# Last section of a one-core transformer kernel in a new order: TensorE transposes for the last tile, results of the last but one pair on ScalarE and GpSimd

## The chip, the cores and the metric

The kernel runs on one core of one Trainium2 chip. A core has five engines that run their own instruction streams side by side: TensorE (PE in the profile, with its weight loads as PEld), VectorE (DVE), ScalarE (ACT), GpSimd (POOL) and SyncE (SP), which here only issues DMAs. They meet through semaphores. PSUM is TensorE's accumulator memory; SBUF is the working memory. The metric is the device time of one execution in microseconds (us), as the median of several runs; lower is better.

## What is computed

The reference takes 64 sequences of 64 tokens of width 1024, adds an attention block to them, and then adds a quantized feed-forward block. Only the second part matters here:

```python
z   = x @ W.T + SCALING * lora(x)                # "cond2", 4096 tokens x 1024
def dynamic_quant(v, inv_smooth):                # one scale for each token
    s = v * inv_smooth
    scale = maximum(max(abs(s), axis=-1) / 127, 1e-8)
    return clip(round(s / scale), -127, 127), scale
qg, sg = dynamic_quant(bf16(z), inv_gate)        # over 1024 columns
qu, su = dynamic_quant(bf16(z), inv_up)
g = (qg @ w_gate.T) * sg * s_wgate               # 512 columns
u = (qu @ w_up.T)   * su * s_wup
inter = bf16(clip(silu(g) * u, -10, 10))
qi, si = dynamic_quant(inter, inv_inter)         # over 512 columns
out = x + (qi @ w_down.T) * si * s_wdown         # 1024 columns
```

## The kernel before

The 4096 tokens are 32 tiles of 128 tokens, and two tiles make a pair; there are 16 pairs. The second stage (`second_stage`) handles one pair after another, and the steps of neighbouring pairs are interleaved by hand. The order of the Python calls is the order of the instructions on each engine: the block runs under a manual schedule, so an instruction that waits holds up everything behind it on its engine. Semaphores follow from which tile each instruction reads and writes. A tile comes from a pool with a number of buffers for each tag, taken in turn; the first write into a buffer that is used again waits until every reader of the tile that had it before is done, and a DMA counts as done when it has landed.

The steps of one tile, with the lines that the profile gives them:

- `undivided` / `completed` (L1487, L1463): TensorE makes z in PSUM. `rounded` (L1497): ScalarE writes it to SBUF as bf16.
- `quant_a`: VectorE multiplies by the smoothing row (L1531), takes the largest absolute value (L1535), and `scaled_down` makes the scale and its reciprocal (L1559, L1561); ScalarE then rounds in two passes (L1562, L1564). `quant_half` / `quant_whole` (L1546, L1547, L1553) do the same for a tile whose two halves of 512 columns come at different times.
- `quant_b`: VectorE clips (L1572). The operand is then turned, either by a transposing DMA that SyncE issues (L1575) or, with `by_pe`, by TensorE into PSUM (L1579), from where ScalarE copies it (L1580).
- `gate_or_up` (L1589): eight matmuls. `scaled` (L1594): VectorE applies the scales, and for the gate ScalarE takes the sigmoid (L1600). `glu` (L1606, L1607, L1609): three VectorE instructions. Then `quant_a` and `quant_b` once more for "i", with 512 columns.
- `down` (L1619): two times four matmuls. `result` (L1628): VectorE multiplies a half tile from PSUM by the token's scale and the column scale in one instruction. Without an adder, GpSimd then issues an accumulating DMA of the whole tile into the output (L1636), where x already stands. With an adder, x is added from SBUF (L1632, on GpSimd or VectorE), and SyncE stores each half (L1633).

The change lies in the straight-line section at the end of the stage, from L1699. There p is the last pair, q the last but one, r the one before that. Names in the text such as "q0" or "p1" are a pair and its tile (0 or 1); "the last tile" is p1. When the stretch in question begins, at 2370.5 us of the span, TensorE has just finished the last base product (the second half of p1). What is left then: both operands of p1, their gate and up matmuls, the glu of p0 and p1, and the down matmuls and results of q0, q1, p0 and p1.

Buffers that the steps speak of: pool `q3` has two buffers for each tag. In the kernel before, the results of q0 and q1 use tag "y"; the results of p0 and p1 use tag "q", in which q_g and q_u of the last tile stood before them. In the new function `result_by_act` the results of q0 and q1 have tag "q" too. The PSUM pools `ps_g` and `ps_h` have four banks each.

Of the kernel before, what the change touches and what calls it, by code (L numbers as in the profile page):

```python
# [11 lines left out]
F32 = mybir.dt.float32  # L12
# [3 lines left out]
AF = mybir.ActivationFunctionType  # L16
ALU = mybir.AluOpType
AX = mybir.AxisListType
PSUM = bass.MemoryType.PSUM

P = 128
# [1264 lines left out]
def second_stage(tc, a, out_t, xT_d, ident, ps_g, KC, NT, H, C, half, comb, op):  # L1286


    nc = tc.nc
# [7 lines left out]
    hs = [slice(0, HH), slice(HH, H)]  # L1297

    with ExitStack() as ctx:
# [7 lines left out]
        def load_row(name, src, n, pool=None):  # L1307
            t = (pool or w).tile([P, n], F32, tag=name, name=name)
            nc.sync.dma_start(t, bcast_rows(src))
            return t  # L1310
# [35 lines left out]
        p2 = ctx.enter_context(tc.tile_pool(name="q3", bufs=2, reuse_waits="tile"))  # L1346
# [3 lines left out]
        st = st1  # L1350
# [12 lines left out]
        sd_w = load_row("sd_w", a["s_wdown"], H)  # L1363
# [131 lines left out]
        def rounded(p, t, n):  # L1495
            s = st[p]
            nc.scalar.copy(s["z"][:, t, hs[n]], s.pop(("ps", t, n)))  # L1497
# [22 lines left out]
            elif i == 3:  # L1520
                nc.vector.tensor_tensor(z[:, 1, hs[0]], ps, s.pop("u2"), ALU.add)

        def quant_a(p, t, nm, between=None):

            s = st[p]
            src, inv, n = {
                "g": (lambda: s["z"][:, t, :], ig, H), "u": (lambda: s["z"][:, t, :], iu, H),
                "i": (lambda: s.pop(("inter", t)), ii, I),
            }[nm]
            q = p2.tile([P, n], F32, tag="q" + ("i" if nm == "i" else ""), name=f"q_{nm}_{p}_{t}")  # L1530
            nc.vector.tensor_tensor(q, src(), inv, ALU.mult)  # L1531
            if between:
                quant_b(*between)
            am = sm.tile([P, 1], F32, tag="am" + nm, name=f"am_{nm}_{p}_{t}")
            nc.vector.tensor_reduce(am, q, AX.X, ALU.max, apply_absolute_value=True)  # L1535
            scaled_down(p, t, nm, q, am, n)

        def quant_half(p, t, nm, n):

            s = st[p]  # L1540
            inv = ig if nm == "g" else iu
            if n == 0:
                s["q", nm] = p2.tile([P, H], F32, tag="q", name=f"q_{nm}_{p}_{t}")
                s["am", nm] = sm.tile([P, 2], F32, tag="amh" + nm, name=f"amh_{nm}_{p}_{t}")
            q = s["q", nm][:, hs[n]]
            nc.vector.tensor_tensor(q, s["z"][:, t, hs[n]], inv[:, hs[n]], ALU.mult)  # L1546
            nc.vector.tensor_reduce(s["am", nm][:, n:n + 1], q, AX.X, ALU.max, apply_absolute_value=True)  # L1547

        def quant_whole(p, t, nm):
            s = st[p]  # L1550
            q, am2 = s.pop(("q", nm)), s.pop(("am", nm))
            am = sm.tile([P, 1], F32, tag="am" + nm, name=f"am_{nm}_{p}_{t}")
            nc.vector.tensor_tensor(am, am2[:, 0:1], am2[:, 1:2], ALU.max)  # L1553
            scaled_down(p, t, nm, q, am, H)

        def scaled_down(p, t, nm, q, am, n):
            s = st[p]
            sc = s["sc", nm, t] = sm.tile([P, 1], F32, tag="sc" + nm, name=f"sc_{nm}_{p}_{t}", bufs=4)
            nc.vector.tensor_scalar(sc, am, 1.0 / QMAX, 1e-8, ALU.mult, ALU.max)  # L1559
            rs = sm.tile([P, 1], F32, tag="rs" + nm, name=f"rs_{nm}_{p}_{t}")  # L1560
            nc.vector.reciprocal(rs, sc)  # L1561
            nc.scalar.activation(q, q, AF.Copy, bias=MAGIC, scale=rs)  # L1562
            qb = s["qb", nm, t] = p2.tile([P, n], BF16, tag="qb" + nm, name=f"qb_{nm}_{p}_{t}")
            nc.scalar.activation(qb, q, AF.Copy, bias=-MAGIC)  # L1564

        def quant_b(p, t, nm, by_pe=False):


            s = st[p]
            n = I if nm == "i" else H  # L1570
            qb = s.pop(("qb", nm, t))
            nc.vector.tensor_scalar(qb, qb, QMAX, -QMAX, ALU.min, ALU.max)  # L1572
            s["qT", nm, t] = qT = p2.tile([P, n // P, P], BF16, tag="qT" + nm, name=f"qT_{nm}_{p}_{t}")
            if not by_pe:
                nc.sync.dma_start(qT, qb, transpose=True)  # L1575
                return
            ps = ps_g.tile([P, n // P, P], BF16, tag="g", name=f"qTp_{nm}_{p}_{t}")
            for c in range(n // P):
                nc.tensor.transpose(ps[:, c, :], qb[:, c * P:(c + 1) * P], ident_b)  # L1579
            nc.scalar.copy(qT, ps)  # L1580

        def gate_or_up(p, t, nm):
            s = st[p]
            qT = s.pop(("qT", nm, t))

            pool, tag = (ps_g, "g") if (p, t) == (NPAIR - 1, 1) else (ps_h, "h")
            ps = s["pgu", nm, t] = pool.tile([P, I], F32, tag=tag, name=f"p{nm}_{p}_{t}")
            for k in range(KC):
                nc.tensor.matmul(ps, qT[:, k, :], wt_b["w" + nm][:, k, :], start=(k == 0), stop=(k == KC - 1))  # L1589

        def scaled(p, t, nm):
            s = st[p]
            o = p1p.tile([P, I], F32, tag="o" + nm, name=f"o{nm}_{p}_{t}")
            nc.vector.scalar_tensor_tensor(  # L1594
                o, s.pop(("pgu", nm, t)), s.pop(("sc", nm, t)), sg_w if nm == "g" else su_w, ALU.mult, ALU.mult
            )
            s["o", nm, t] = o
            if nm == "g":
                e = p1p.tile([P, I], F32, tag="e", name=f"e_{p}_{t}")
                nc.scalar.activation(e, o, AF.Sigmoid)  # L1600
                s["e", t] = e

        def glu(p, t):
            s = st[p]
            e, g, u = s.pop(("e", t)), s.pop(("o", "g", t)), s.pop(("o", "u", t))
            nc.vector.tensor_mul(e, g, e)  # L1606
            nc.vector.tensor_mul(e, e, u)  # L1607
            inter = p1p.tile([P, I], BF16, tag="inter", name=f"inter_{p}_{t}")
            nc.vector.tensor_scalar(inter, e, LIMIT, -LIMIT, ALU.min, ALU.max)  # L1609
            s["inter", t] = inter  # L1610

        def down(p, t):
            s = st[p]
            qT = s.pop(("qT", "i", t))
            for n in range(2):
                pool, tag = (ps_g, "g") if p == NPAIR - 1 else (ps_h, "h")
                ps = s["pd", t, n] = pool.tile([P, HH], F32, tag=tag, name=f"pd_{p}_{t}_{n}")
                for k in range(IC):
                    nc.tensor.matmul(  # L1619
                        ps, qT[:, k, :], wt_b["wd"][:, k, hs[n]], start=(k == 0), stop=(k == IC - 1)  # L1620
                    )

        def result(p, t, *adds):
            s = st[p]
            y = p2.tile([P, H], F32, tag="q" if p == NPAIR - 1 else "y", name=f"y_{p}_{t}")
            si = s.pop(("sc", "i", t))
            for n in range(2):
                nc.vector.scalar_tensor_tensor(  # L1628
                    y[:, hs[n]], s.pop(("pd", t, n)), si, sd_w[:, hs[n]], ALU.mult, ALU.mult
                )  # L1630
                if adds:
                    adds[n % len(adds)].tensor_add(y[:, hs[n]], y[:, hs[n]], s["x", t][:, hs[n]])  # L1632
                    nc.sync.dma_start(out_t[2 * p + t, :, hs[n]], y[:, hs[n]])  # L1633
            if not adds:

                nc.gpsimd.dma_start(out_t[2 * p + t], y, accum_op=ALU.add)  # L1636

        def do(when, f, *args):
# [5 lines left out]
        for p in range(NPAIR - 1):  # L1644
            q, r = p - 1, p - 2
# [6 lines left out]
            do(last, down, r, 0)  # L1652
            token_sums(p)
            do(last, quant_a, r, 1, "i")
            base(p, 1)
            after(p, 1)
# [42 lines left out]
        p, q, r = NPAIR - 1, NPAIR - 2, NPAIR - 3  # L1699
# [44 lines left out]
        glu(q, 1)  # L1744
        gate_or_up(p, 0, "g")
        rounded(p, 1, 1)
        quant_half(p, 1, "g", 0)
        quant_half(p, 1, "u", 0)
        gate_or_up(p, 0, "u")
        quant_half(p, 1, "g", 1)  # L1750
        quant_whole(p, 1, "g")
        quant_b(q, 0, "i")
        quant_half(p, 1, "u", 1)
        quant_whole(p, 1, "u")
        down(q, 0)
        quant_b(p, 1, "g")
        quant_a(q, 1, "i")
        scaled(p, 0, "g")
        scaled(p, 0, "u")
        quant_b(p, 1, "u")  # L1760
        gate_or_up(p, 1, "g")
        glu(p, 0)
        quant_b(q, 1, "i")
        gate_or_up(p, 1, "u")
        quant_a(p, 0, "i")
        scaled(p, 1, "g")
        scaled(p, 1, "u")
        down(q, 1)
        quant_b(p, 0, "i", True)
        glu(p, 1)  # L1770
        quant_a(p, 1, "i")
        result(q, 0)
        down(p, 0)
        quant_b(p, 1, "i", True)
        result(q, 1, nc.gpsimd)
        result(p, 0, nc.gpsimd, nc.vector)
        down(p, 1)
        result(p, 1, nc.vector)
# [54 lines left out]
```

## Time and profile before

| | us |
|---|---|
| median of 3 runs | 2402.47 (2402.36 to 2408.15) |
| the execution that was profiled, its own time | 2406.19 |
| its span, first to last instruction | 2404.4 |
| TensorE busy | 2367.6 (98% of the span) |
| VectorE busy | 1334.5 (56%) |
| ScalarE busy | 936.2 (39%) |
| GpSimd busy | 418.7 (17%) |
| end of the last base product | about 2370.5 |
| end of the last VectorE instruction | 2397.71 |

Start times below are counted from the start of the span. A timeline row gives the start, the duration, the engine, the line of the kernel, the operation, and output and inputs by the program's names, with shapes; in brackets stands how long the engine had been idle before it and what ended that.

### The profile page before, as it was taken

Reading aid. Unit: us, or ns where it says so; the run is one execution under the profiler, and the core shown is the slowest. Engines: PE = TensorE matmul, PEld = TensorE weight load, DVE = VectorE, ACT = ScalarE, POOL = GpSimd, SP = SyncE. Lnnn points to the kernel's source line nnn. Section 1 sums busy time; section 2 is a strip of 40 time slices with the busy share of each in tenths; the row PEclk is TensorE's granted clock in tenths of the full one; section 3 lists DMA queues with packets and bytes.
Section 4 is the critical chain, followed back from the end, with each engine's and each line's share of the span. In section 5 each row is a group of like instructions: output and inputs, shape, how many; then the busy total and the mean of one; then the engine's idle time right before and its main releaser. Section 6 shows DMA issues by size and latency. Waiting matters only on the chain.

```text
span 2404.4 us, 41907 instructions
## 1 busy us (share of the span) xinstructions
PE 2367.6 (98%) x17066; PEld 1628.5 (68%) x17104; DVE 1334.5 (56%) x2584; ACT 936.2 (39%) x1220; POOL 418.7 (17%) x470
## 2 busy tenths in 40 slices
PE   8999999999999999999999999999999999999997
PEld 7888888888888888888888444444454545454452
DVE  3573474464543644633535533324377878777787
ACT  1344344343344443443434544343333333333333
POOL 4121112111122223220000333334100000000000
PEclk9999999999999999999999999999999999999999
DMA  7899799899899998997967788877733443444353
GB/s 229 217 240 248 190 228 241 221 232 220 208 232 274 212 255 230 242 237 179 207 188 196 213 257 258 275 218 248 239 77 75 90 79 83 84 86 82 70 119 76
DMA packets 612395, 453.84 MB, mean 189 GB/s; under 512 B 362465, under 2 KB 524258, under 8 KB 606690
## 3 DMA queue, kind: packets, MB, share of 16 engines
q1 hardware_dynamic: 581522, 393.91, 63.2%
q0 software_dynamic: 12240, 40.38, 7.9%
q10 hardware_dynamic: 18432, 16.79, 3.1%
q8 instruction: 137, 2.24, 0.4%
q14 instruction: 64, 0.52, 0.1%
HBM read 274.02 MB, written 91.23 MB: 152 GB/s over the span
## 4 chain that ended last, share of the span: by engine, by line
PE 92%; DMA 2%; DVE 1%; SPq 1%; issue 1%; ACT 0%; ACTq 0%; DVEq 0%
PE poa L1129 5%; PE poc L1129 5%; PE pod L1129 5%; PE psvc L530 4%; PE psva L530 4%; PE psvd L530 4%; PE pbc L1129 4%; PE pbd L1129 4%; PE pba L1129 4%; PE pskc L509 4%; PE pskd L509 4%; PE pska L509 4%; PE psqa L509 4%; PE psqd L509 4%; PE psqc L509 4%; PE pr L1398 2%
## 5 line engine op out<-in xcount | busy, mean ns | idle before, releaser
L582 ACT ACTIVATE prob<-prob 128x512 f32<-128x512 f32 x128 | 80.6, 629 | 346.7 <-DVE prob L578 338.6
L608 ACT COPY pT<-phT 128x1024 int16<-128x1024 int16 x128 | 165.4, 1339 | 25.4 <-DMA phT<-ph 21.4
L596 ACT COPY ph<-prob 128x1024 int16<-128x1024 int16 x128 | 133.5, 1043 | 63.1 <-DVE prob L590 38.4
L442 POOL COPY yB<-yhT 128x512 int16<-128x512 int16 (+1 forms) x84 | 75.8, 955 | 426.4 <-DMA yhT<-yh 426.4
L1636 POOL DMA_DIRECT2D out_dram<-y x29 | 25.2, 869 | 656.2 <-DVE y L1628 644.4
L577 DVE TENSOR_REDUCE mx<-s 128x8 f32<-128x512 f32 x128 | 87.4, 682 | 71.6 <-PE s L568 71.6
L1250 POOL TENSOR_TENSOR xo<-xo,ob 128x1024 f32<-128x1024 f32 x32 | 83.5, 2629 | 228.2 <-DVE prob L578 189.5
L509 PE MATMUL psqa<-yB,wq 128*128 128x256 f32 x512 | 121.1, 379 | 0.5 <-ACT psqp L479 0.5
L509 PE MATMUL pska<-yB,wk 128*128 128x256 f32 x512 | 120.9, 379 | 0.0
L1224 ACT COPY xh<-xo 128x1024 int16<-128x1024 int16 x64 | 64.4, 1041 | 142.8 <-DVE xo L1269 142.8
L530 PE MATMUL psva<-wv,yB 128*128 128x256 f32 x512 | 115.8, 379 | 0.0
L1129 PE MATMUL poa<-woA,cx 128*128 128x512 f32 x256 | 115.3, 593 | 0.0
L1129 PE MATMUL pba<-wtA,x1T 128*128 128x512 f32 x240 | 107.9, 592 | 0.0
L1235 ACT COPY xTo<-xhT 128x1024 int16<-128x1024 int16 x64 | 84.7, 1337 | 58.4 <-DMA xhT<-xh 53.3
L530 PEld LDWEIGHTS psva<-wv,yB 128*128 128x128 f32 x512 | 97.2, 190 | 14.0 <-issue 0.8
L509 PEld LDWEIGHTS psqa<-yB,wq 128*128 128x128 f32 x512 | 97.1, 190 | 14.0 <-ACT psqp L479 0.9
L509 PEld LDWEIGHTS pska<-yB,wk 128*128 128x128 f32 x512 | 97.3, 190 | 13.2
L633 ACT ACTIVATE co<-banks,bqkv 128x256 f32<-128x256 f32 x128 | 60.7, 474 | 109.3 <-PE banks L411 79.8
L1266 POOL TENSOR_TENSOR xo<-xo,ou 128x512 f32<-128x512 f32 x48 | 59.9, 1275 | 191.8 <-DVE ou L1263 191.8
L590 DVE TENSOR_TENSOR prob<-prob,den 128x512 f32<-128x512 f32 x128 | 89.4, 699 | 4.4
L578 DVE TENSOR_TENSOR prob<-s,mx 128x512 f32<-128x512 f32 x128 | 88.5, 691 | 4.5
L1129 PEld LDWEIGHTS poa<-woA,cx 128*128 128x128 f32 x256 | 48.5, 190 | 60.0 <-issue 59.5
(255 smaller groups left out, 4945.8 us busy)
## 6 DMA issues: line engine op xcount, KB each, us to landing
wv<-v_d SPq DMA_DIRECT2D x56, 512.0 KB
wq<-q_d SPq DMA_DIRECT2D x28, 1024.0 KB
wk<-k_d SPq DMA_DIRECT2D x28, 1024.0 KB
wq<-in_qkvw_dram SPq DMA_DIRECT2D x100, 256.0 KB
wk<-in_qkvw_dram SPq DMA_DIRECT2D x100, 256.0 KB
wv<-in_qkvw_dram SPq DMA_DIRECT2D x50, 512.0 KB
x<-in_x_dram SPq DMA_DIRECT2D x32, 512.0 KB
ctx_d<-co ACTq DMA_DIRECT2D x128, 128.0 KB
```

Of the source, the lines that this page charges most:

```text
L442: nc.gpsimd.tensor_copy(dst, src[:, :, :, halves[r] if hf else r])
L509: nc.tensor.matmul(ps[:, 0:HB], A[:, SLOT[A_OF[i]], k, :], B[B_OF[i]][:, k, :], start=first and k == 0, stop=k == KQ - 1, skip_group_check ...
L530: nc.tensor.matmul(ps[:, j * VC:(j + 1) * VC], B[B_OF[i]][:, k, j * P:(j + 1) * P], A[:, k, :], start=first and j == 0 and k == 0, stop=k ...
L577: nc.vector.tensor_reduce(mx, ps[:, :, n, :, :], AX.X, ALU.max)
L578: nc.vector.tensor_tensor(p.rearrange("p j h k -> p h j k"), ps[:, :, n, :, :], mx.unsqueeze(3).to_broadcast([P, HPC, 2, C]), ALU.subtract,)
L582: nc.scalar.activation(p, p, AF.Exp, scale=scale)
L590: nc.vector.tensor_tensor(p, p, den.unsqueeze(2).to_broadcast([P, n, C]), ALU.mult)
L596: nc.scalar.copy(h, planes(p.rearrange("p n k -> p (n k)")))
L608: nc.scalar.copy(planes(pT.rearrange("p a b q -> p (a b q)")), hT)
L1129: self.nc.tensor.matmul(ps, self.B[self.B_OF[i]][:, k, :], self.A[self.A_OF[i]][:, k, :], start=first and k == 0, stop=k == self.KQ - 1, s ...
L1235: nc.scalar.copy(planes(xT.rearrange("p k q -> p (k q)")), hT)
L1250: nc.gpsimd.tensor_add(s["x"][:, t, :], s["x"][:, t, :], self.ob)
```

## The change

It touches only the end section and the helpers that it calls. The main loop calls `quant_b` and `quant_a` with arguments that give the same instructions as before.

- The clip and the transposing DMA of q0's "i" operand are issued ahead of the second half of the last tile's quantization.
- Two smoothing products (the second half of p1's "u", and q1's "i") are issued on GpSimd. The maximum of a half can be issued apart from its product (`half_maximum`).
- Both operands of p1, "g" and "u", are turned by TensorE, eight 128x128 transposes each, right behind their clips, instead of by DMA. VectorE copies the one out of PSUM, ScalarE the other.
- The results of q0 and q1: ScalarE multiplies PSUM by the token's scale, GpSimd multiplies by the column scale and, for q1, adds x. VectorE has no part in them. They come earlier in the order, q0's ahead of `down(q, 1)`.

```diff
-        def quant_a(p, t, nm, between=None):
+        def quant_a(p, t, nm, between=None, eng=nc.vector):
...
-            nc.vector.tensor_tensor(q, src(), inv, ALU.mult)
+            eng.tensor_tensor(q, src(), inv, ALU.mult)
...
-        def quant_half(p, t, nm, n):
+        def quant_half(p, t, nm, n, eng=nc.vector):
...
-            nc.vector.tensor_tensor(q, s["z"][:, t, hs[n]], inv[:, hs[n]], ALU.mult)
-            nc.vector.tensor_reduce(s["am", nm][:, n:n + 1], q, AX.X, ALU.max, apply_absolute_value=True)
+            eng.tensor_tensor(q, s["z"][:, t, hs[n]], inv[:, hs[n]], ALU.mult)
+            s["am2", nm, n] = lambda: nc.vector.tensor_reduce(
+                s["am", nm][:, n:n + 1], q, AX.X, ALU.max, apply_absolute_value=True
+            )
+
+        def half_maximum(p, nm, n):
+            st[p].pop(("am2", nm, n))()
...
-        def quant_b(p, t, nm, by_pe=False):
+        def quant_b(p, t, nm, by_pe=None):
...
-            nc.scalar.copy(qT, ps)
+            by_pe(qT, ps)
...
+        def result_by_act(p, t, add):
+
+            s = st[p]
+            y = p2.tile([P, H], F32, tag="q", name=f"y_{p}_{t}")
+            si = s.pop(("sc", "i", t))
+            for n in range(2):
+                nc.scalar.activation(y[:, hs[n]], s.pop(("pd", t, n)), AF.Copy, scale=si)
+                nc.gpsimd.tensor_tensor(y[:, hs[n]], y[:, hs[n]], sd_w[:, hs[n]], ALU.mult)
+                if add:
+                    nc.gpsimd.tensor_add(y[:, hs[n]], y[:, hs[n]], s["x", t][:, hs[n]])
+                    nc.sync.dma_start(out_t[2 * p + t, :, hs[n]], y[:, hs[n]])
+            if not add:
+                nc.gpsimd.dma_start(out_t[2 * p + t], y, accum_op=ALU.add)
...
         gate_or_up(p, 0, "g")
         rounded(p, 1, 1)
-        quant_half(p, 1, "g", 0)
-        quant_half(p, 1, "u", 0)
+        for nm in ("g", "u"):
+            quant_half(p, 1, nm, 0)
+            half_maximum(p, nm, 0)
+        quant_b(q, 0, "i")
         gate_or_up(p, 0, "u")
+        quant_half(p, 1, "u", 1, nc.gpsimd)
         quant_half(p, 1, "g", 1)
+        half_maximum(p, "g", 1)
         quant_whole(p, 1, "g")
-        quant_b(q, 0, "i")
-        quant_half(p, 1, "u", 1)
+        half_maximum(p, "u", 1)
         quant_whole(p, 1, "u")
+        quant_a(q, 1, "i", None, nc.gpsimd)
         down(q, 0)
-        quant_b(p, 1, "g")
-        quant_a(q, 1, "i")
+        quant_b(p, 1, "g", nc.vector.tensor_copy)
+        quant_b(p, 1, "u", nc.scalar.copy)
         scaled(p, 0, "g")
         scaled(p, 0, "u")
-        quant_b(p, 1, "u")
         gate_or_up(p, 1, "g")
+        quant_b(q, 1, "i")
         glu(p, 0)
-        quant_b(q, 1, "i")
+        quant_a(p, 0, "i")
         gate_or_up(p, 1, "u")
-        quant_a(p, 0, "i")
         scaled(p, 1, "g")
         scaled(p, 1, "u")
+        quant_b(p, 0, "i", nc.scalar.copy)
+        glu(p, 1)
+        result_by_act(q, 0, False)
         down(q, 1)
-        quant_b(p, 0, "i", True)
-        glu(p, 1)
         quant_a(p, 1, "i")
-        result(q, 0)
         down(p, 0)
-        quant_b(p, 1, "i", True)
-        result(q, 1, nc.gpsimd)
+        result_by_act(q, 1, True)
+        quant_b(p, 1, "i", nc.scalar.copy)
         result(p, 0, nc.gpsimd, nc.vector)
         down(p, 1)
         result(p, 1, nc.vector)
```

## Prediction

> **What bounds the kernel now.** I read the shares of the engines first, then the granted clock (full until 2392), then the busy times cut into the stretches of the last 34 us, then the chain that ended last, and last the timelines of each engine there. The change touches nothing before 2368.8 us, so only this end can move. Its stretches (start:end, length, busy time and instructions of PE, PEld, DVE, ACT, POOL, then clock, DMA share, GB/s):
>
> ```profile
> 2370.50:2375.00 4.50, 3.44 (x16) 1.37 (x14) 3.57 (x10) 2.34 (x3) 0.00 (x0) 1.00 0.09 18
> 2375.00:2380.00 5.00, 2.82 (x13) 1.15 (x14) 4.32 (x11) 4.42 (x6) 0.00 (x0) 1.00 0.33 63
> 2380.00:2385.00 5.00, 3.48 (x17) 1.41 (x16) 4.41 (x10) 1.56 (x3) 0.00 (x0) 1.00 0.42 79
> 2385.00:2390.50 5.50, 3.03 (x17) 1.30 (x15) 5.16 (x11) 2.25 (x4) 0.00 (x0) 1.00 0.00 0
> 2390.50:2397.80 7.30, 3.27 (x12) 1.09 (x12) 7.10 (x10) 0.59 (x1) 5.03 (x4) 0.65 0.78 179
> 2397.80:2404.40 6.60, 0.00 (x0) 0.00 (x0) 0.00 (x0) 0.00 (x0) 0.00 (x0) 0.50 0.38 135
> ```
>
> TensorE, 98% busy over the whole span, is not the bound here; VectorE is nearly full from 2375 on. TensorE does wait, and the timeline shows for what:
>
> ```profile
> 2375.86 1.90 PE L1619 MATMUL pd<-wd,qT_i 128*128 128x512 bf16 x8 [1.88 <-DMA qT_i<-qb_i]
> 2379.08 1.90 PE L1589 MATMUL pg<-wg,qT_g 128*128 128x512 bf16 x8 [1.32 <-ACT qb_i L1564]
> 2382.50 1.90 PE L1589 MATMUL pu<-wu,qT_u 128*128 128x512 bf16 x8 [1.52 <-DMA qT_u<-qb_u]
> 2390.86 0.40 PE L1579 MATMUL qTp_i<-ident_b,qb_i 128*128 128x128 bf16 x4 [1.93 <-DVE qb_i L1572]
> ```
>
> The first three are waits for transposing DMAs (the second names ScalarE, which was done; its operand landed then), 4.7 us together. The change removes just these. But the chain of waits passes only the third, and from 2384.4 on it runs through VectorE alone. One more thing must be read before GpSimd gets work beside VectorE:
>
> ```profile
> 1417.28 2.87 POOL L1250 TENSOR_TENSOR xo<-xo,ob 128x1024 f32<-128x1024 f32 x1 [2.67 <-issue]
> 1417.86 2.83 DVE L1142 TENSOR_TENSOR To<-cx,To 128x512 f32<-128x512 f32 x1
> ...
> 2393.48 1.18 DVE L1632 TENSOR_TENSOR y<-y,x_ll 128x512 f32<-128x512 f32 x1
> 2394.07 1.71 POOL L1632 TENSOR_TENSOR y<-y,x_ll 128x512 f32<-128x512 f32 x1
> 2395.35 0.98 DVE L1632 TENSOR_TENSOR y<-y,x_ll 128x512 f32<-128x512 f32 x1
> ```
>
> A VectorE product of two SBUF tiles, 0.69 us alone, ends 0.55 us after the GpSimd product that runs beside it: 1420.15 to 1420.69, and 2395.78 to 2396.33. GpSimd in turn takes 1.71 instead of 1.26 where it starts behind such a VectorE instruction. They take turns. The VectorE form with one operand in PSUM (L1628) keeps its 0.74 us.
>
> **How I sum.** I followed each engine's queue in program order from 2370.5 with the durations of the rows (0.03 us between dependent instructions; neighbours that don't depend overlap by 0.09) and this taking of turns. For the order of before that gives 2397.6 as the end of the last VectorE instruction; the profile has 2397.7. The same walk with the new order:
>
> 1. *q0's "i" operand ahead.* Its clip (0.27) takes a VectorE gap at 2368.8, and its DMA lands in 2.46 (2373.40 to the matmul at 2375.86), at 2371.5, on an SP queue empty since 2364. `down(q, 0)` runs at 2373.8, the 1.88 us wait goes. TensorE is late next on the clip of "g" at 2375.9, which is as before. Worth 0 to the end.
> 2. *Two products on GpSimd.* 128x512 takes 1.26 there in float32; a bf16 operand is in no row, so 1.0 to 1.71, I take 1.27. The first starts beside VectorE's own product and ends at 2373.0, the second at 2374.3; VectorE reaches their maxima at 2373.1 and 2374.4. ScalarE is busy with "g" until 2375.4, so 1 us of delay would be hidden. 0.
> 3. *TensorE turns "g" and "u".* Four transposes took 0.40, so eight take 0.65 to 0.80; I take 0.65. VectorE's copy of 128x1024 bf16 out of PSUM is in no row: from 0.42 (the clip of that shape, SBUF) to 1.22 (two times a VectorE copy of 128x512 out of PSUM, 0.69, less the start); I take 1.22, nearest in memory. "g" lies in SBUF at 2377.8, 1.1 earlier than by DMA. The clip of "u" follows at 2377.7 (ScalarE delivers at 2377.6), 0.7 earlier than before. ScalarE's copy is 1.01 (128x1024 int16 out of PSUM, L420).
> 4. *What that copy delays.* It stands ahead of p0's sigmoid on ScalarE: 2378.9 to 2379.9, sigmoid until 2380.4, before 2379.55. The glu of p0, its quantization, p1's sigmoid and the glu of p1 all hang on it: +0.8, so the glu of p1 starts at 2386.1 instead of 2385.35. "u" of p1 is now ready at 2382.3, 2.1 earlier, but it is no longer last. The removed TensorE waits are thus worth nothing, and the step costs 0.8.
> 5. *q0's results beside the glu of p1.* ScalarE's scaling out of PSUM is 0.585 (copy) plus 0.10 (a pointer operand, L633 against L479): 0.69. Its first half ends at 2387.5, GpSimd takes the port at 2387.6, and VectorE's product for p1's "i" (due 2388.0, normally over at 2388.7) ends at 2389.7: +1.0. If both of GpSimd's products come ahead of it, it is +2.5; if it is ahead of both, 0. I take 1.0, the order that the times give.
> 6. p1's "i" operand leaves ScalarE at 2392.2 (before 2390.5). The rest of its way, clip, transposes, copy, `down`, is over by 2396; ScalarE's two q1 halves hold the copy up by 0.4.
> 7. *q1's results, the new last link.* ScalarE takes them behind that operand, so GpSimd starts at 2392.9 and does four steps of 1.27: second half ready at 2398.1, store issued. The results of all four tiles share tag "q" with two buffers, so the result of p1 waits for both q1 stores to land, and that of p0 for q0's accumulating DMA (5.5 us by its row, at 2396.5, covered). A 256 KB store: the last two of before took 4.0 from the second's issue (2398.3) to SyncE's closing waits (2402.3); less 0.8 for one store at the 340 GB/s of then, 3.2. The bounds are 2.46 (transposing DMA) and 5.5. So VectorE starts p1's results at 2401.4 instead of 2394.6.
> 8. Four instructions, 2.83: the last ends at **2404.2**, before 2397.7, +6.5. Behind VectorE stand here only the stores.
> 9. *Tail.* Before, 6.7: SyncE was 0.55 late (a store's issue took 1.47), landing 4.0, closing 2.1. Now 0.05 + 3.2 + 2.1 = 5.35 (up to 6.7). Span 2409.55 against 2404.4: **+5.15**. Against the profiled execution (2406.19, 1.8 outside the span) that is 2411.3; the median of the runs is 2402.47, so I forecast **2407.6**, +0.21%.
>
> Four VectorE results (4 x 0.74) leave VectorE, but GpSimd's four times 1.27 and a landed store stand in their place.
>
> **Two rules against it.** The rows show the turns only for two SBUF operands. The Trainium skill, "GPSIMD Engine Reference", section "Key points", also lets VectorE instructions in a two-port mode collide with GpSimd; no row here shows it. By that the limiter of the glu (L1609) and the clips would wait too, an estimated 1.5 us more in step 5. And "TensorE: Matmul & The Clock Gate", "Part 4: PE-mode transpose", gives about 275 ns for one transpose in a kernel: eight would be an estimated 2.2 us and the chain of step 4 about 3 us later. The row has four in 0.40, and it decides.
>
> **Rivals.**
> - *The buffer chain is longer (slower).* Place: GpSimd's four q1 steps and the landing of their store. If each step takes the 1.71 of the contended row and the store the 5.5 of the other DMA that carries y, that adds 4 x 0.42 + 2.3 = 3.9 to 4.0: **2411.5**. It decides the sign once the stretch from 2392.9 to the landing exceeds 8.4 + 2.1 = 10.5 us. For it: VectorE's additions for p0 and the accumulating DMA fall in there. Against: the DMA share is near nothing at that time.
> - *No wait for the buffer.* Then VectorE is done by 2398.2, but GpSimd's addition for p0, last in its queue, ends at 2400.7, and SyncE sends four stores behind it: 1 MB at 340 GB/s, 3.1 us, plus some 2.3 of start and landing, plus 2.1: 2408.2, +3.8: **2406.3**. Against: one tag with two buffers for four results.
> - *The change does what its words suggest (faster).* If TensorE's three waits were the bound, 4.7 us go: **2397.8**. Against: VectorE's 4.32 of 5.00, 4.41 of 5.00 and 5.16 of 5.50 in the stretches where they lie.
>
> **How the numbers follow.** About 0.3% (7.2 us, 2409.7) is what a measurement of this kernel can tell from no change. Forecast 2407.6: 0.52 (own range 2405.5 to 2409.7). No buffer wait: 0.13. Both end within 0.3%: 0.65. Longer chain: 0.28, slower. TensorE bound: 0.07, faster. The range runs from 2404.5 (no buffer wait, with step 5 at nothing and a landing shorter by 0.75) to 2412.8 (forecast, +1.5 for the port, +2.3 for the landing, +1.35 for the tail), which leaves out the faster case and a little of the slowest.
>
> **What would show it.** Step 1: no DMA wait in front of `down(q, 0)`. Steps 3 and 4: eight transposes within 0.8 us, p0's sigmoid at about 2379.8 behind ScalarE's copy. Step 5: a VectorE product of 1.6 us or more beside GpSimd's first q0 product. Step 7: VectorE idle for about 2.7 us ahead of the first L1628 of p1, released by a DMA out of y. If that idle time is missing, step 7 is wrong; if p1's "i" operand leaves ScalarE before 2390.5, steps 4 and 5 are.

## The result, and the profile after

The changed kernel takes 2410.73 us (median of 9 runs, 2408.26 to 2416.81); the kernel before, run beside it, 2403.86 (9 runs, 2399.72 to 2408.15). The ratio is 1.0025, 95% interval 1.0014 to 1.0036: slower by a quarter of a per cent, inside the forecast range of 2404.5 to 2412.8, though above the narrower 2405.5 to 2409.7 that the forecast gave as its own. The profiled execution took 2411.39, its span is 2409.6 (before 2404.4).

Not all of that difference belongs to the change. The last base product ended at 2371.50 in this execution and at 2370.55 in that of before, and in the profiles of the experiments anywhere from 2363 to 2376, with the same instructions ahead of it. So I measure the section by its own length from here on: the **stretch** from the end of the last base product to the end of the span. Before 33.85, after 38.10: **+4.25**; the other 0.95 of the +5.2 came earlier. "At 15.80" below means 15.80 us behind that base product.

For comparison, two rows of before: p0's sigmoid, and VectorE's product for p1's "i".

```profile
2378.94 0.61 ACT L1600 ACTIVATE e<-og 128x512 f32<-128x512 f32 x1
...
2387.26 0.69 DVE L1531 TENSOR_TENSOR q_i<-inter,ii 128x512 f32<-128x512 bf16 x1
```

From the timeline of after (start, duration, engine, line, operation, tiles, and the idle time ahead of it), one row for each step of the prediction:

```profile
2377.04 0.62 PE L1584 MATMUL qTp_g<-ident_b,qb_g 128*128 128x128 bf16 x8 [0.38 <-DVE qb_g L1577]
...
2377.70 0.69 DVE L1585 COPY qT_g<-qTp_g 128x1024 bf16<-128x1024 bf16 x1 [0.72 <-PE qTp_g L1584]
...
2379.17 0.84 PE L1584 MATMUL qTp_u<-ident_b,qb_u 128*128 128x128 bf16 x8 [1.51 <-DVE qb_u L1577]
...
2379.80 3.39 PE L1594 MATMUL pg<-wg,qT_g 128*128 128x512 bf16 x8
...
2380.04 1.01 ACT L1585 COPY qT_u<-qTp_u 128x1024 bf16<-128x1024 bf16 x1
...
2380.95 0.63 ACT L1605 ACTIVATE e<-og 128x512 f32<-128x512 f32 x1
...
2388.81 3.16 POOL L1650 TENSOR_TENSOR y<-y,sd_w 128x512 f32<-128x512 f32 x2 [13.84 <-ACT y L1649]
2389.21 1.64 DVE L1531 TENSOR_TENSOR q_i<-inter,ii 128x512 f32<-128x512 bf16 x1
...
2397.99 1.41 DVE L1633 SCALAR_TENSOR_TENSOR y<-pd,sc_i,sd_w 128x512 f32<-128x512 f32 x2 [4.29 <-DMA out_dram<-y]
...
2401.69 0.75 DVE L1633 SCALAR_TENSOR_TENSOR y<-pd,sc_i,sd_w 128x512 f32<-128x512 f32 x1 [0.73 <-DMA out_dram<-y]
```

Both operands are turned early and TensorE waits for no DMA. But the sigmoid of p0 stands behind ScalarE's copy, VectorE's product for p1's "i" takes 1.64 instead of 0.69 beside GpSimd's, and VectorE then sits idle twice, 4.29 and 0.73, each time until a DMA out of y has landed. TensorE's last matmul ended at 2398.66, 3 us before VectorE read its result, so TensorE is not the last link. The chain of waits (start, length, what) ends so:

```profile
2392.28 5.59 DMA out_dram<-y
...
2397.94 1.27 POOL y L1652
...
2399.22 2.35 DMA out_dram<-y
...
2401.69 0.76 DVE y L1633
```

Read it upwards. VectorE's last results wait for a store of q1; this store for GpSimd's last q1 addition; and the chain credits that to q0's accumulating DMA, which landed 0.07 before it began; but GpSimd's step ahead of it had itself ended at 2397.85, so its steps stand back to back there. The real path at this place is GpSimd's four steps, the store, VectorE's last results. The windows from 2390.5 on (columns as before) say the same with the engines' shares: VectorE 1.65 busy of 7.30, where before it had 7.10, and 5.58 of 6.60 where before it had nothing.

```profile
2390.50:2397.80 7.30, 3.82 (x14) 1.39 (x12) 1.65 (x5) 2.98 (x5) 6.04 (x5) 0.68 0.54 89
2397.80:2404.40 6.60, 0.86 (x3) 0.00 (x0) 5.58 (x7) 0.00 (x0) 2.54 (x3) 0.50 0.47 171
```

### The profile page after: what moved, and what is told of

Its sections match the earlier page's. It is cut to its first block, busy times and chain, and to the rows that moved or that the text cites. A ratio compares the mean times of both kernels' runs of the same rounds, so it can differ in the third digit from the quotient of the medians.

```text
span 2409.6 us, 41984 instructions
## 1 busy us (share of the span) xinstructions
PE 2373.5 (99%) x17120; PEld 1630.0 (68%) x17120; DVE 1334.0 (55%) x2579; ACT 940.0 (39%) x1225; POOL 427.0 (18%) x476
## 4 chain that ended last, share of the span: by engine, by line
PE 91%; DVE 2%; DMA 1%; ACT 1%; issue 1%; SPq 1%; ACTq 0%; POOL 0%; DVEq 0%; POOLq 0%
PE poa L1129 5%; PE poc L1129 5%; PE pod L1129 5%; PE psvc L530 4%; PE psva L530 4%; PE psvd L530 4%; PE pbc L1129 4%; PE pbd L1129 4%; PE pba L1129 4%; PE pskd L509 4%; PE pskc L509 4%; PE pska L509 4%; PE psqa L509 4%; PE psqd L509 4%; PE psqc L509 4%; PE pr L1398 2%
```

## The experiments

Theory: the section is longer by the results of q0 and q1 on GpSimd with their shared buffers (+3.2 to 3.6) and by ScalarE's copy ahead of the sigmoid (+0.8 to 1.1). Rivals: the two-engine clash at VectorE's product is the main loss; or the early transposes are a gain that the results hide. A difference of 1 us is 0.04% of the time, which no median here resolves, so the verdicts rest on the stretch of one profiled execution each; the medians are given beside it. The ratio, with its 95% interval, is as recorded; it is not the quotient of the two medians.

| kernel | stretch | last VectorE instruction ends at | median; before beside it; ratio |
|---|---|---|---|
| before | 33.85 | 27.16 | |
| after | 38.10 | 33.05 | 2410.73; 2403.86; 1.0025 [1.0014, 1.0036] |
| e1_tag_y | 37.78 | 27.57 | 2407.82; 2404.92; 1.0 [0.9989, 1.0012] |
| e2_vector_results | 34.91 | 27.91 | 2406.38; 2404.92; 1.0006 [0.9994, 1.0018] |
| e3_results_only | 37.83 | 32.59 | 2409.96; 2404.92; 1.0015 [1.0003, 1.0027] |
| e4_dma_ahead_only | 33.77 | 27.16 | 2405.87; 2404.92; 1.0007 [0.9992, 1.0022] |
| e5_sigmoid_first | 34.00 | 26.98 | 2399.05, one run; 2402.72 |
| e6_q1_accumulated | 37.05 | 29.68 | 2412.93, one run; 2402.72 |
| e7_q0_results_late | 40.59 | 35.63 | 2409.35, one run; 2405.63 |
| e8_p0_added_by_vector | 37.54 | 28.57 | 2409.11, one run; 2405.63 |
| f1_gaps_filled | 34.15 | 26.88 | 2403.19; 2402.72; 1.0003 [0.9993, 1.0012] |
| f2_gaps_q1_accumulated | 34.67 | 27.06 | 2403.85; 2402.72; 1.0001 [0.999, 1.0012] |
| f3_down_behind_up | 33.83 | 27.05 | 2403.18; 2405.63; 0.999 [0.9979, 1.0] |
| f4_gate_before_u | 32.42 | 25.41 | 2403.1; 2403.82; 0.9999 [0.9987, 1.0011] |

### The change taken apart

**e2_vector_results**: the changed kernel with the results of q0 and q1 as before.

```diff
-        result_by_act(q, 0, False)
         down(q, 1)
         quant_a(p, 1, "i")
+        result(q, 0)
         down(p, 0)
-        result_by_act(q, 1, True)
         quant_b(p, 1, "i", nc.scalar.copy)
+        result(q, 1, nc.gpsimd)
```

> The changed kernel with the results of q0 and q1 on VectorE again, in the places they had before the change (q1's addition on GpSimd); transposes by TensorE, the two products on GpSimd and the DMA of q0's operand ahead all stay. Mine: the glu of p1 starts 15.8 us after the last base product (14.8 before), because p0's sigmoid still stands behind ScalarE's copy; from there the old end follows, so the stretch is 34.6 to 35. Rival (TensorE's three DMA waits were the bound): they are gone, so the stretch falls well below 33.85, to 29 to 32.

Stretch 34.91. Everything but the results costs 1.06; no hidden gain comes out. The glu of p1 starts at 15.59 (before 14.80, after 15.80).

**e3_results_only**: the kernel before, with only those two calls, and `down(q, 1)` behind the first of them, in the places of after.

```diff
-        down(q, 1)
         quant_b(p, 0, "i", True)
         glu(p, 1)
+        result_by_act(q, 0, False)
+        down(q, 1)
         quant_a(p, 1, "i")
-        result(q, 0)
         down(p, 0)
+        result_by_act(q, 1, True)
         quant_b(p, 1, "i", True)
-        result(q, 1, nc.gpsimd)
```

> The kernel before with nothing but the results of q0 and q1 moved to ScalarE and GpSimd, in the places of the changed kernel; operands of the last tile still turned by DMA. Mine: the glu of p1 starts as before (14.8 us after the last base product), then the product beside GpSimd costs 0.9 and the chain of GpSimd's four steps and the landed stores follows; 37.0 to 37.4. Rival (the transposes and the lower TensorE clock that they bring are the loss): 33.9 to 34.5.

Stretch 37.83: +3.98 of the +4.25, where 37.0 to 37.4 was expected. The two idle times are there again (4.14 and 1.18), and so is the slow product (1.71). The parts add up to 5.04, more than the whole. GpSimd's steps for q1 start 0.93 earlier here than in after (21.60 against 22.53), but the store behind them took longer to land: VectorE's last results begin only 0.47 earlier (29.72 against 30.19). Whether that is more than chance, one execution of each can't say.

**e4_dma_ahead_only**: the kernel before, with `quant_b(q, 0, "i")` moved from ahead of the second half of "u" to ahead of `gate_or_up(p, 0, "u")`.

> The kernel before with only the clip and transposing DMA of q0's operand moved ahead. Mine: TensorE's wait of 1.88 us in front of the first down matmuls goes, the stretch stays at 33.85 within 0.3. Rival (TensorE's waits are the bound): 32.0.

Stretch 33.77: nothing. The wait that TensorE loses in front of `down(q, 0)` it gets back in front of p1's gate matmuls, 3.36 instead of 1.32. These then ran at a lowered clock, 3.37 instead of 1.90, and even that did not lengthen the stretch:

```profile
2377.76 3.37 PE L1589 MATMUL pg<-wg,qT_g 128*128 128x512 bf16 x8 [3.36 <-ACT qb_i L1564]
```

**e5_sigmoid_first**: e2 with one line moved, so that p0's sigmoid comes ahead of ScalarE's copy.

```diff
         quant_b(p, 1, "g", nc.vector.tensor_copy)
+        scaled(p, 0, "g")
         quant_b(p, 1, "u", nc.scalar.copy)
-        scaled(p, 0, "g")
         scaled(p, 0, "u")
```

> The second experiment (results on VectorE, stretch 34.91) with p0's gate scaled, and so its sigmoid issued, ahead of the clip and copy of "u" instead of behind them. Mine (step 4: the loss in front of the glu of p1 is p0's sigmoid standing behind ScalarE's copy): the glu of p1 starts 0.8 to 1.1 us earlier than the 15.6 of that experiment, the stretch is 33.8 to 34.2. Rival (the loss is the lateness of the last tile's operands themselves): "u" comes 0.4 later by this, so the stretch grows to 35.2 or so.

Stretch 34.00, as expected: 0.91 of the 1.06 is that copy. The glu of p1 starts at 14.66, earlier than before (14.80).

### Which link of the results decides

**e1_tag_y**: in `result_by_act`, `tag="q"` becomes `tag="y"`, so that no result of p waits for a store of q.

> The changed kernel with one word different: the results of q0 and q1 take tag "y" as before the change, so the results of p0 and p1 find free buffers. I measure the stretch from the end of the last base product to the end of the span: 33.85 us before the change, 38.1 after. Buffer theory (mine): VectorE's 4.3 us and 0.7 us of waiting for a DMA out of y vanish, its first result of p0 stands right behind the last clip, and the last link becomes GpSimd's addition for p0 with four stores behind it; 36.5 to 37. Rival (TensorE's halved clock: its last eight matmuls take 3.6 us instead of 2.9): the results of p1 wait for those instead and the stretch stays within 0.4 of 38.1.

VectorE's two waits for DMAs are gone and it ends 5.5 earlier, at 27.57, and yet the stretch is 37.78, only 0.32 shorter. That is the rival's figure, but not for the rival's reason: here TensorE's last eight matmuls ran at full clock, in 1.90. From the timeline of e1 (VectorE, GpSimd and SyncE's queue):

```profile
2390.46 0.80 DVE L1637 TENSOR_TENSOR y<-y,x_ll 128x512 f32<-128x512 f32 x1
2390.78 1.60 POOL L1652 TENSOR_TENSOR y<-y,x_l 128x512 f32<-128x512 f32 x1
...
2395.77 1.25 POOL L1637 TENSOR_TENSOR y<-y,x_ll 128x512 f32<-128x512 f32 x1
...
2397.05 2.52 SPq L1638 DMA_DIRECT2D out_dram<-y  x4
```

Three of GpSimd's four steps for q1, now beside VectorE's additions, take 1.59 to 1.79 instead of 1.26; its addition for p0, last in its queue, ends at 29.9; and behind it SyncE sends four stores, which take it to the end. A second link was nearly as late as the first. The size of this rests on one execution: +3.93 over before would be 0.16% of the time, and the recorded ratio of e1, 1.0 [0.9989, 1.0012], does not show it.

**e6_q1_accumulated**: e1 with `result_by_act(q, 1, False)`: GpSimd multiplies only, and x is added by an accumulating DMA as for q0.

> The first experiment (results of q0 and q1 in tag "y", stretch 37.78) with x added to q1 by an accumulating DMA, as for q0, instead of by two GpSimd additions. If GpSimd's queue is the last link once the buffers are free (new theory): two steps of about 1.6 us leave it, the addition for p0 ends about 2.4 us earlier, level with VectorE's last instruction, and the stretch is 34.3 to 35.0. Rival (the stores and their bandwidth end the span whatever GpSimd does): the same bytes move, and an accumulating DMA takes longer; 37.5 to 38.5.

37.05, by neither account. GpSimd's addition for p0 ended at 27.7, 2.2 earlier than in e1, but VectorE's addition took 2.23 beside it, and 7.37 passed behind the last VectorE instruction. **e8_p0_added_by_vector** took that clash away: `result(p, 0, nc.vector)`.

> The kernel of e6_q1_accumulated (tag y for the results of q0 and q1, q1 accumulated by DMA) with both additions for p0 on VectorE instead of one of them on GpSimd. Nothing is left out. e6: stretch 37.05, last VectorE instruction ended at 29.68 after the base product, of which VectorE's addition waited 1.54 for GpSimd's addition beside it, and 7.37 from there to the end of the span, four stores being issued behind GpSimd's addition. Theory (with the buffer wait gone, GpSimd's queue is the last link: its addition for p0 holds VectorE's and the stores behind it on SyncE): the last VectorE instruction ends at 27.0 to 28.2, the time behind it falls to 5.3 to 6.3, stretch 32.8 to 34.3. Rival (the accumulating DMA of q1, or the matmuls of p1 at the lower clock, set the end): the stretch stays at 35.5 to 37.

My theory falls: VectorE ends 1.1 earlier, and yet the stretch is 37.54, even longer than the rival's 35.5 to 37. From the timeline of e8, the issue of q1's accumulating DMA and the last VectorE instruction:

```profile
2395.21 0.88 POOL L1655 DMA_DIRECT2D out_dram<-y  x1 [0.30 <-POOL y L1650]
...
2397.54 0.69 DVE L1637 TENSOR_TENSOR y<-y,x_ll 128x512 f32<-128x512 f32 x1
```

That DMA took 6.3 to land, so until 2401.5, and the span ended 5.7 later. In e6 it was issued at the same place (25.56, in e8 25.55), landed after 5.8, and the span ended 5.7 later too. It looks as if the accumulating DMA set the end by itself. It doesn't: stores by SyncE go out beside it and are still moving data when it has landed, as two windows of e8 show (columns as before; the last two figures are the DMA engines' busy share and GB/s):

```profile
2401.50:2403.70 2.20, 0.00 (x0) 0.00 (x0) 0.00 (x0) 0.00 (x0) 0.00 (x0) 0.50 0.33 102
2403.70:2407.20 3.50, 0.00 (x0) 0.00 (x0) 0.00 (x0) 0.00 (x0) 0.00 (x0) 0.50 0.02 5
```

The DMA records give the same for every kernel here: the span ends 2.6 to 3.6 behind the last data of the stores (3.2 in before, 3.5 in e8, 2.6 in e6). In e8 that data ends 5.1 behind the issue of the last store, in the kernels with one accumulating DMA 1.5 to 3.7. From 2398.3 until the landing the DMA engines were 0.97 busy, so the stores had to share them with the accumulating DMA. That fits the account of e6's rival, the stores and their bandwidth; no run takes only the second accumulating DMA away, so its part is not shown by itself.

**e7_q0_results_late**: the changed kernel with `result_by_act(q, 0, False)` moved behind `quant_a(p, 1, "i")`, so that GpSimd is free when VectorE's product comes.

> The changed kernel with one step moved: the results of q0 (ScalarE, GpSimd, accumulating DMA) behind VectorE's product and maximum for p1's operand i, instead of ahead of them. Nothing is left out. Changed kernel: stretch 38.10, the product for p1's operand i took 1.64 beside GpSimd's first product, that operand left ScalarE at 21.9 after the base product. Theory (that product waits for GpSimd's whole instruction): the product takes 0.69, the operand leaves ScalarE at about 20.9, but GpSimd's chain of six steps starts about 1 us later and moves into the time of the results, and with the shared buffers the accumulating DMA and the stores land later by as much or more: stretch 38.3 to 40.5. Rival A (the clash at the port is the main loss of the change): stretch 37.0 to 37.4. Rival B (the product is slow for another reason than GpSimd's instruction beside it): the product stays at 1.5 or more.

From the timeline of e7:

```profile
2384.40 0.69 DVE L1531 TENSOR_TENSOR q_i<-inter,ii 128x512 f32<-128x512 bf16 x1
...
2396.58 1.41 DVE L1633 SCALAR_TENSOR_TENSOR y<-pd,sc_i,sd_w 128x512 f32<-128x512 f32 x2 [8.64 <-DMA out_dram<-y]
```

The product is back at 0.69 and the operand leaves ScalarE at 20.71 (after 21.88), yet the stretch is 40.59, 2.5 longer and just past the upper end expected: GpSimd starts later, its accumulating DMA lands later, and VectorE waits 8.64 for the buffer. The clash is real and worth about 1 us to that operand, but the chain through GpSimd decides.

### Versions meant to beat both

**f1_gaps_filled** (against the changed kernel) goes back to VectorE's results, with q1's "i" quantized in VectorE's early gaps, the sigmoid ahead of the copies, and nothing new on GpSimd:

```diff
         quant_b(q, 0, "i")
+        quant_a(q, 1, "i")
         gate_or_up(p, 0, "u")
-        quant_half(p, 1, "u", 1, nc.gpsimd)
...
         quant_whole(p, 1, "g")
+        quant_b(q, 1, "i")
+        quant_half(p, 1, "u", 1)
...
-        quant_a(q, 1, "i", None, nc.gpsimd)
         down(q, 0)
-        quant_b(p, 1, "g", nc.vector.tensor_copy)
+
+        def scaled_and_copied(qT, ps):
+            scaled(p, 0, "g")
+            nc.vector.tensor_copy(qT, ps)
+
+        quant_b(p, 1, "g", scaled_and_copied)
+        down(q, 1)
         quant_b(p, 1, "u", nc.scalar.copy)
-        scaled(p, 0, "g")
         scaled(p, 0, "u")
...
         scaled(p, 1, "g")
+        quant_a(p, 0, "i")
         scaled(p, 1, "u")
+        glu(p, 1)
         quant_b(p, 0, "i", nc.scalar.copy)
```

> A version built from the findings: TensorE turns the last tile's operands as in the change; nothing is multiplied on GpSimd; q1's "i" quantization fills VectorE's 2 us gap ahead of the last half tile; the sigmoids stand ahead of ScalarE's copies; p1's gate is scaled ahead of p0's "i" quantization; the results of q0 and q1 are on VectorE, in the gaps where it waits for the last operand. Mine (VectorE's chain and then its results set the end): the glu of p1 starts about 13.5 us after the last base product (14.8 before), the last VectorE instruction is over at 25.8 (27.16 before), the stretch is 32.5. Rival (stores set the end): 33.5 to 34.

34.15, where 32.5 was expected: just past the rival's 33.5 to 34. VectorE waited 1.50 for p1's gate matmuls: the second half of `down(q, 1)` waited 1.10 for a PSUM bank, and the transposes of "u" stood behind it. **f2_gaps_q1_accumulated** has q1's x added by DMA on top (`result(q, 1)`):

> The version before this in the list, but x is added to q1 by an accumulating DMA instead of on GpSimd. Mine: GpSimd adds only p0's first half, at most one VectorE addition meets it, so VectorE is over about 0.5 us earlier than there and the stretch is 32.0, as long as the longer DMA (5.6 us from its issue at about 20.5) lands inside the tail. Rival (the bandwidth of the accumulating DMA delays the last stores): 33 to 34.

34.67: no shorter, and past the rival's 33 to 34 too. The wait stays. q1's accumulating DMA, issued at 2391.01, took 7.4 to land, and the stores' data ended 2.6 behind that.

**f3_down_behind_up** moves `down(q, 1)` behind `gate_or_up(p, 1, "u")`.

> The order of f1_gaps_filled with one step moved: both halves of q1's down matmuls stand behind p1's up matmuls instead of ahead of the transposes of u. Nothing is left out. Compared by the stretch from the end of the last base product (the start of the last half tile that ScalarE rounds, less 0.02) to the end of the span, 34.15 in f1, 33.85 in the kernel before. Theory (in f1 VectorE waited 1.50 for p1's gate matmuls because the second half of q1's down held the transposes of u up for 1.10 until VectorE had emptied a PSUM bank): the transposes of u start right behind their clip at 7.7 instead of 9.1 after the base product, the gate matmuls of p1 end by 10.2, VectorE starts the gate scaling at about 10.1 with less than 0.3 of idle time instead of 1.50, the glu of p1 starts at 13.1 instead of 14.5, and the stretch is 32.6 to 33.0. That is 1 us under before, too little for the ratio of medians to show (1.000 within 0.0015). Rival (q1's down, now later, holds the results up, or the gate matmuls start at a lowered clock): the idle time in front of VectorE's results or of the gate scaling stays over 1 us and the stretch 33.8 to 34.5.

33.83: the gate matmuls start at 8.2 as expected and VectorE still waits 1.68 for them, because they take 3.36 instead of 1.89. From its timeline, and from its windows (columns as before; clock third from the end):

```profile
2375.21 0.88 PE L1584 MATMUL qTp_u<-ident_b,qb_u 128*128 128x128 bf16 x8 [1.51 <-ACT e L1605]
...
2375.88 3.36 PE L1594 MATMUL pg<-wg,qT_g 128*128 128x512 bf16 x8
...
2379.28 0.75 DVE L1599 SCALAR_TENSOR_TENSOR og<-pg,sc_g,sg_w 128x512 f32<-128x512 f32 x1 [1.68 <-PE pg L1594]
```

```profile
2375.00:2376.00 1.00, 0.79 (x9) 0.79 (x10) 1.00 (x3) 0.22 (x1) 0.00 (x0) 0.71 0.00 0
2376.00:2377.00 1.00, 1.00 (x4) 0.34 (x3) 0.97 (x2) 0.88 (x1) 0.00 (x0) 0.50 0.00 0
```

**f4_gate_before_u** (f1 again, with `down` taking the halves that it is to do) puts half of `down(q, 1)` where TensorE had waited, and the gate matmuls ahead of the transposes of "u":

```diff
         quant_b(p, 1, "g", scaled_and_copied)
-        down(q, 1)
+        down(q, 1, (0,))
+        gate_or_up(p, 1, "g")
         quant_b(p, 1, "u", nc.scalar.copy)
         scaled(p, 0, "u")
-        gate_or_up(p, 1, "g")
         glu(p, 0)
         gate_or_up(p, 1, "u")
+        down(q, 1, (1,))
```

> The order of f1_gaps_filled with TensorE's queue of the section changed: transposes of g, first half of q1's down, gate matmuls of p1, transposes of u, up matmuls of p1, second half of q1's down. The other engines' orders stay. Nothing is left out. Compared by the stretch from the end of the last base product to the end of the span: f1 34.15 (gate matmuls of p1 start 9.5 after the base product, VectorE waits 1.50 for them), f3_down_behind_up 33.83 (start 8.2, but 3.36 instead of 1.89 long, VectorE waits 1.68), before 33.85. Theory (f3 gained nothing because the gate matmuls ran at a lowered clock, in front of which TensorE had waited 1.51; here real work, the half of down, stands there): the gate matmuls start at about 7.1 and take 1.9, VectorE's gate scaling of p1 follows the glu of p0 without waiting, its up scaling starts at 12.6 to 12.9 instead of 13.8 and the stretch is 32.8 to 33.2; ratio of medians 0.9990 to 1.0002. Rival (the lowered clock hits the matmuls here as well): the gate or the up matmuls take 3 or more, and the stretch is 33.7 to 34.6.

The gate matmuls take 1.89 at 6.9, VectorE takes p1's gate without waiting, and its row shows no idle time:

```profile
2379.91 1.89 PE L1594 MATMUL pg<-wg,qT_g 128*128 128x512 bf16 x8
...
2382.83 0.74 DVE L1599 SCALAR_TENSOR_TENSOR og<-pg,sc_g,sg_w 128x512 f32<-128x512 f32 x1
```

Stretch 32.42, below the 32.8 to 33.2 expected and the shortest of all: 1.43 less than before and 5.7 less than after. Against before its median gives 0.9999 [0.9987, 1.0011]; a gain of 0.06% can be read from the section alone.

## Why the forecast held, and where its terms were off

The forecast was +5.15 in the section, the profile has +4.25. The median alone would not tell the forecast from its rivals: 2410.73 lies nearest to the 2411.5 of the longer buffer chain, and +4.25 nearer to the +3.8 of no buffer wait. What decides are the rows. The longer chain needed steps of 1.71 and a landing of 5.5, and they took 1.26 and 2.35; the rival without a buffer wait needed VectorE to find its buffers free, and it waited for both. The 3.1 by which the median exceeds the forecast do not come from the section: 2402.47 and the +4.25 would give 2406.7, the median of before was itself 1.39 higher this time, and the ratio's interval allows 3.4 to 8.7. That the total lies inside the range is therefore in part luck; the section is the better test. (The 0.42 that the longer chain adds for a contended step should be 0.44 or 0.45 by its own rows, which moves it by 0.1.) By its steps:

- *Steps 1 and 2, nothing.* Right. TensorE takes `down(q, 0)` without a wait; e4 alone gives 33.77 against 33.85. GpSimd's products took 1.66 and 1.15 and were covered.
- *Step 3.* VectorE's copy out of PSUM was mis-sized: 1.22 taken, 0.69 measured. It costs nothing, since ScalarE delivers "u" later than that. Eight transposes took 0.62 and, with the clock falling, 0.84: 0.08 to 0.1 each, not the 275 ns that the Trainium skill ("TensorE: Matmul & The Clock Gate", "Part 4: PE-mode transpose") gives for one.
- *Step 4, +0.75 to 0.8 at the glu of p1.* Right in place and size: +0.78 in e1, e2, e6, e7 and e8 (15.58 or 15.59 against 14.80); after has +1.00, of which 0.2 is the lowered clock under the transposes of "u". e5 shows the cause.
- *Step 5, +1.0 for the turn-taking.* Right: 1.64 against 0.69, +0.95, and 0.69 again in e7 where GpSimd is idle. The extra 1.5 by the two-port rule didn't come, but in no run's section did the limiter or a clip start behind a GpSimd product that was already running, so the rule itself is untested here.
- *Step 7, the new last link.* Right in mechanism. GpSimd's four steps took 1.26 each, from 22.53 to 27.69 (predicted 22.35 to 27.55). The landing was mis-sized: 3.2 taken, 2.35 measured. With it VectorE began p1's results at 30.2 instead of 30.85 and ended at 33.05 instead of 33.65. That q0's accumulating DMA would be covered was only half so: VectorE waits for it first, 4.29, and just 0.73 is left for the store, where the forecast's sign was about 2.7: p0's results began 0.5 later than forecast, VectorE's addition took 1.53 beside GpSimd's, and the store landed early. Without the store it would be nearly as late.
- *Step 9.* The tail was 5.05 instead of 5.35. The 0.6 and this 0.3 are the 0.9 that the forecast was too high.
- *"No buffer wait", +3.8.* Priced right: +3.93 in the one profile of e1, with VectorE done at 27.57 (forecast 27.65) and GpSimd's addition for p0 at 29.90 (30.15). The forecast put GpSimd's steps and the wait for a landed store together as the new link; the wait alone is worth 0.32 there. The loss is GpSimd's work behind p1's operand, with whatever DMA follows it: without the buffers it is the four stores (e1), and with q1 added by DMA that DMA and the stores beside it (e6, e8).
- *"Does what its words suggest."* TensorE's three waits were not the bound: without them, and without the results, the section is 1.06 longer (e2). Whether they were worth something with VectorE's queue mended is not shown: f4, which keeps the early operands, is 1.43 shorter than before, but it also has VectorE's queue in a new order, and no run has that order without the early operands.

## What to carry to other kernels

Taking work off the busiest engine shortens nothing if the engine that gets it is slower, starts behind the same operand and ends in a DMA that an engine or the end of the program waits for: add up the new chain to the landing and to the next user of the buffer. Near the end of a program, count every queue from its last item to the end, since removing the latest link gains only the distance to the second. And where an engine's wait is removed, see which of its later instructions then stands in front of the wait.

## What the runs showed of the hardware

- *TensorE's clock can fall within the section.* In after, the windows from 2379 to 2383 have the clock at 0.71, 0.50, 0.50 and 0.58: full speed halved for 3.42 us (0.29, 0.50, 0.50 and 0.42 lost, by 0.5). The gate matmuls of p1 under it took 3.36 to 3.47 (after, e4, e5, e6, f3), else 1.89 or 1.90. It came after gaps such as the 1.51 ahead of the transposes of "u", but not in every execution: after, e1, e2, e6, e7 and e8 issue the same instructions on TensorE up to there, and only after and e6 ran the gate matmuls at the lower clock. The Trainium skill ("TensorE: Matmul & The Clock Gate", "Part 1: The HAM clock gate") has a free-running window of 3413 ns, which agrees: in each of the 14 traces the recorded changes of the clock lie a whole number of 3.413 us apart. Cut into these windows, the section shows more: behind every window at full clock in which TensorE was busy for a share of 0.37 or less the clock fell, behind every one with 0.5 or more it stayed, and in between both happened (it fell behind 0.45 in after and stayed behind 0.48 in e1). f3 and f4 make a pair: their windows end at the same place, 7.76, after 1.65 and 3.12 us busy of 3.41, and the clock fell in f3 alone. So the work within a window matters, and where the windows lie differs from one execution to the next; each version's clock was seen in one execution only.
- *An accumulating DMA of 512 KB is dear:* 5.3 to 7.4 from issue to landing in this section (5.3 in e2, 7.4 in f2), where a store of 256 KB took 2.35 in after. In e6, e8 and f2, which issue two, the stores beside them end later: their data ended 4.0, 5.1 and 4.2 behind the issue of the last store, against 1.5 to 3.7 in the kernels that issue one. Some 3 us then pass to the end of the span in every kernel (2.6 to 3.6); what happens in them stays open.
- *VectorE copies 128x1024 bf16 out of PSUM in 0.69*, the time of 128x512 float32; GpSimd's product with a bf16 operand takes 1.15, against 1.26 in float32.
- *GpSimd and VectorE slow each other both ways:* beside the other's additions GpSimd's steps took 1.59 to 1.79 instead of 1.26 (e1), VectorE's additions 1.53 (after), 1.70 (e3) and 2.23 (e6) instead of 0.69.
